# A graph network on one core: the first pass in slots of 60 columns, with larger evictions, two terms for all pieces, and the norm in batches

## The chip, the cores and the metric

One core of one Trainium2 chip runs the whole program. The metric is device time in microseconds of one execution. The engines are TensorE (PE, with its weight loads shown apart as PEld), VectorE (DVE), ScalarE (ACT), GpSimd (POOL) and SyncE (SP, which issues most DMAs). Each runs its own instructions in order and waits for the others by semaphores.

## The reference

A graph has 6250 nodes with 128 features and 206250 directed edges. Cut to what matters:

```python
h = jnp.maximum(_layernorm(x), 0.0)
feat = h * power(clip(deg, 1), -0.5)          # deg: edges that leave a node
x = x + relu(segment_sum(feat[src], dst)) @ W0.T + b0

h = jnp.maximum(_layernorm(x), 0.0)
msg = h[src] @ W_msg.T + b_msg + edge_embed[clip(edge_type, 0, 8)]
x = x + gru_cell(segment_sum(msg, dst), h)    # W_ih, W_hh, b_ih, b_hh
```

So there are two sums over edges. In each, a node's row is the sum of the rows of its sources.

## The kernel before

**Idea.** Nodes are padded to 6272 = 49 blocks of 128. The adjacency matrix (how many edges go from source s to destination d) is built on the chip in bf16, and each sum over edges is a dense product of a table of node rows with it. The first pass builds the matrix, uses it for the first layer and stores it to DRAM (`adj_d`); the second pass reads it back in pieces. If counts at the end show that edges were lost, a general path runs instead; it does not run here.

**Prologue** (0 to about 110 us). Edges are sorted into windows: one window holds two destinations, with up to 64 edges each on one half of the partitions. For every edge the low seven bits of its source (`lo_t`) and its block number (`code_t`) are laid out by window. Degrees and the first norm give the table `tab1`, in seven pieces of 7 blocks (CB = HP = 7). Rows are fp32, and their product with the small integers of the matrix is to be nearly exact, so a row is split into terms. `terms_of` (L737) makes three bf16 terms for piece 0 (`NARROW = 1`, `SPL = 3`) and two fp32r terms for pieces 1 to 6.

**First pass** (L803 to L931). Destinations are taken in chunks (`FRONT`): one of 128 columns and 24 of 256. Its steps:

- `hots` (L343, operations recorded at L336): DVE compares 32 windows (`TW`) with an iota, to `hot_l` (128 x 32 x 128) and `hot_c` (128 x 32 x 50).
- `build` (L812): for each destination PE multiplies the two one-hots on its half of the partitions, 64 rows by 128 by 49 (L823); the result is that destination's column of the matrix, as 128 x 49. Sixteen of them fill a tile `ev` of two PSUM banks, of which there are three buffers. ACT evicts 784 elements per partition at a time to bf16 `adj` (L832).
- `cast` (L893, recorded at L896): pieces 1 to 6 of a finished chunk are cast to fp32r `wide1` (three buffers), on ACT and DVE in turn. Piece 0 is multiplied as bf16 directly.
- `sums` (L780, products at L791): for each block and term one product, 128 x 128 by 256 columns, all 105 into one accumulator `acc`.
- `first_layer` (L837): Relu on ACT (L842), the product with `w0_sb` on PE (L847, in the other half of the accumulator's bank), then on DVE the bias (L851), the residual (L852), the norm's statistics and aggregate (L857, L858), on ACT a square root (L860), on DVE its reciprocal and the shift (L861, L862).

The order on PE, ACT and DVE is written out by hand (`manual_schedule`). While chunk c is built in eight rounds of 32 columns (`RUN`), the products of chunk c - 1 are given out in eight parts: in each round come first the 32 small products, then the evictions, then the casts that `cast_at` names, then a step of the layer, then 13 or 14 long products. At the end of a chunk SP is given the DMA that stores its `adj` (L929); the two `adj` buffers alternate, so chunk c + 2 must wait for that store.

**Second pass** (L937 on). ACT makes the new normalized rows (L954), DVE their terms `tab2` (L955, L956). For 13 blocks of up to 512 destinations (`BACK`) pieces of the matrix are loaded (L1046), cast by ACT (L1050) or DVE (L1057), with row sums for the check (L1030), multiplied (L791), and the GRU's gates (L982, L994) and the rest follow (L987 to L1027).

Of the kernel before, what the change touches and what calls it, by code (L numbers as in the profile page):

```python
# [31 lines left out]
CB = 7  # L32
# [10 lines left out]
TW = 32  # L43
# [8 lines left out]
NARROW = 1  # L52
# [3 lines left out]
def spread(n, k):  # L56

    return [n * (i + 1) // k for i in range(k)]

# [199 lines left out]
def by_matrix(  # L259
# [48 lines left out]
    xs = const.tile([P, NB, H], F32, name="xs")  # L308
    rstd = const.tile([P, NB], F32, name="rstd")
    sh = const.tile([P, NB], F32, name="sh")  # L310
    b0_b = const.tile([P, H], F32, name="b0_b")
# [31 lines left out]
    def hots(w0, place=None):  # L343
        if place is None:
            pool = hot[next(turns) % 2]
            hot_l = pool.tile([P, TW, P], BF16, name="hot_l")
            hot_c = pool.tile([P, TW, CODES], BF16, name="hot_c")
        else:
            hot_l = place[:, : TW * P].rearrange("p (t n) -> p t n", n=P)
            hot_c = place[:, TW * P : TW * (P + CODES)].rearrange("p (t n) -> p t n", n=CODES)  # L350
        one_hot(hot_l, lo_t[:, w0 : w0 + TW, :], iota)
        one_hot(hot_c, code_t[:, w0 : w0 + TW, :], iota_1)
        return hot_l, hot_c
# [13 lines left out]
    with tc.tile_pool(name="pro", bufs=1) as pro, tc.manual_schedule(engines={mybir.EngineType.DVE}):  # L367
# [120 lines left out]
        for k0 in range(0, NT // P + 1, 4):  # L488
# [39 lines left out]

        tab1_p = early.enter_context(tc.tile_pool(name="tab1_p", bufs=1, side="right"))
        tab1 = [  # L530
            tab1_p.tile([P, SPL, CB, H], BF16, name=f"tab1_{q}")
            if q < NARROW
            else tab1_p.tile([P, 2, CB, H], F32R, name=f"tab1_{q}")
# [8 lines left out]
        nc.sync.dma_start(out=b0_b, in_=b0.partition_broadcast(P))  # L542
# [57 lines left out]
        emb_f, bmsg_f, rest = emb_f[:TYPES, :], bmsg_f[:TYPES, :], rest[:TYPES, :]  # L600
        terms = terms[:TYPES, :].bitcast(BF16).rearrange("t (s n) -> t s n", s=SPL)
# [15 lines left out]
        nc.scalar.copy(rest, both_ps[1][:TYPES, : 3 * H])  # L617
# [5 lines left out]
        def fetch(b0_, nb):  # L623
# [14 lines left out]
            inside = wnd.tile([P, 2, GB * ROWS, HALF], BF16, name="inside", bufs=1)  # L638
# [98 lines left out]
        def terms_of(c):  # L737
            f, tab = f_of.pop(c), tab1[c]
            nc.vector.tensor_scalar(tab[:, 0], f, 0.0, None, op0=ALU.max)
            if c < NARROW:  # L740
                nc.vector.scalar_tensor_tensor(f, f, 0.0, tab[:, 0], op0=ALU.max, op1=ALU.subtract)
                nc.vector.tensor_copy(tab[:, 1], f)
                nc.vector.tensor_tensor(tab[:, 2], f, tab[:, 1], ALU.subtract)
            else:
                nc.vector.scalar_tensor_tensor(
                    tab[:, 1], f, 0.0, tab[:, 0].bitcast(F32), op0=ALU.max, op1=ALU.subtract
                )
# [10 lines left out]
        for s in range(SPL):  # L758
# [3 lines left out]
            for g in range(3):  # L762
                at = 32 * g + s * TYPES
                nc.sync.dma_start(out=emb_s[at : at + TYPES, :], in_=terms[:, s, g * H : (g + 1) * H])
# [7 lines left out]
        early_hots.append(hots(TW, first_place[:, NB * P :]))  # L772
# [31 lines left out]
    with tc.tile_pool(name="adj_even", bufs=1, reuse_waits="tile") as adj_even, tc.tile_pool(  # L804
        name="wide1", bufs=3, reuse_waits="tile"
    ) as wide1p, tc.tile_pool(
        name="ev_ps", bufs=3, space=PSUM, reuse_waits="tile"
    ) as evp, tc.manual_schedule(
# [3 lines left out]
        def build(adj, batch, parts):  # L812

            hot_l, hot_c = batch
            made = []
            for part in parts:

                ps = evp.tile([P, 2, 512], F32, name="ev")
                for j in range(8):
                    t = part * 8 + j  # L820
                    for d in range(2):
                        half = slice(d * HALF, (d + 1) * HALF)
                        nc.tensor.matmul(  # L823
                            ps[:, d, j * NB : (j + 1) * NB],
                            hot_l[half, t, :],
                            hot_c[half, t, :NB],
                            start=True,
                            stop=True,
                        )
                made.append((part, ps))  # L830
            for part, ps in made:
                nc.scalar.copy(  # L832
                    adj[:, :, part * 16 : (part + 1) * 16].rearrange("p n (j d) -> p n j d", d=2),
                    ps[:, :, : 8 * NB].rearrange("p d (j n) -> p n j d", n=NB),
                )

        def first_layer(c, acc):  # L837
            d0, nd = FRONT[c]
            nb = nd // P
            blocks = slice(d0 // P, d0 // P + nb)  # L840
# [4 lines left out]
            ps = acc[:, DC : 2 * DC].rearrange("p (b f) -> p b f", f=H)  # L845
            for k in range(nb):
                nc.tensor.matmul(ps[:, k, :], r[:, k * P : (k + 1) * P], w0_sb, start=True, stop=True)  # L847
            yield
            x2 = xs[:, blocks, :]
            y = work.tile([P, DC // P, H], F32, name="y", bufs=1)  # L850
            nc.vector.tensor_tensor(y[:, :nb], ps[:, :nb], b0_b.unsqueeze(1).to_broadcast([P, nb, H]), ALU.add)  # L851
            nc.vector.tensor_add(x2, x2, y[:, :nb])  # L852
            yield
            st = work.tile([P, DC // P, 6], F32, name="st2")
            mv = work.tile([P, DC // P, 2], F32, name="mv2", bufs=3)
            for k in range(nb):
                nc.vector.bn_stats(st[:, k, :], x2[:, k, :])  # L857
                nc.vector.bn_aggr(mv[:, k, :], st[:, k, :])  # L858
            yield
            nc.scalar.activation(rstd[:, blocks], mv[:, :nb, 1], AF.Sqrt, bias=eps)  # L860
            nc.vector.reciprocal(rstd[:, blocks], rstd[:, blocks])  # L861
            nc.vector.scalar_tensor_tensor(  # L862
                sh[:, blocks], mv[:, :nb, 0], -1.0, rstd[:, blocks], op0=ALU.mult, op1=ALU.mult
            )
# [3 lines left out]
        RUN = 32  # L868
        cast_at = {0: (1, 2), 2: (3,), 3: (4,), 4: (5,), 5: (6,)}
        TOTAL = (NARROW * SPL + (NCH - NARROW) * 2) * HP  # L870
        ROUNDS = DC // RUN
        batches = [d // 2 for d in range(0, NP, 2 * TW)]
        ready = early_hots
        made = len(ready)
        adjs = {}
        before, late = None, iter(())
        NC = len(FRONT)
        for c in range(NC + 1):
            d0, nd = FRONT[c] if c < NC else (NP, 0)
            acc, steps = None, iter(())  # L880
            wide = {}
            if c > 0:
                done = adjs.pop(c - 1)
                n = FRONT[c - 1][1]
                acc, steps = sums(
                    n, tab1, lambda q, done=done, wide=wide: wide[q] if q >= NARROW else done[:, q * HP : (q + 1) * HP]
                )
            if c < NC:
                adjs[c] = (adj_even if c % 2 else adj_odd).tile([P, NB, DC], BF16, name="adj") if c > 0 else adj_first
            rounds = nd // RUN if c < NC else ROUNDS  # L890
            ends = spread(TOTAL, rounds)

            def cast(q):  # L893
                wide[q] = wide1p.tile([P, HP, DC], F32R, name="wide1")
# [3 lines left out]
            for r in range(rounds):  # L898
                casts = cast_at.get(r, ()) if c > 0 else ()
                for q in casts:  # L900
                    if r == 0:
                        cast(q)
# [235 lines left out]
```

## Time and profile before

| | us |
|---|---|
| median of 3 runs | 949.86 (947.5 to 950.5) |
| the profiled execution, its own time | 949.22 |
| its span, first to last instruction | 947.1 |
| PE busy | 873.4 (92%) |
| DVE busy | 816.0 (86%) |
| ACT busy | 733.8 (77%) |
| mean granted TensorE clock | 0.965 |

Busy times are unions: instructions of one engine overlap a little, so a duration is longer than the distance from one start to the next. In rows of the timeline a number before the engine is the start and the next the length of a run of equal instructions; brackets give the idle time before it and what ended it. In the table of stretches the columns are the stretch, its length, busy time and count of PE, PEld, DVE, ACT and POOL, then the granted clock, the DMA share and GB/s. A chain row has start, length and what ran.

### The profile page before, as it was taken

The numbers are of one execution on the slowest core, as the hardware profiler recorded it, in microseconds if no ns is written. First come the engines' busy times: TensorE is split into PE (matmuls) and PEld (weight loads), VectorE is DVE, ScalarE is ACT, GpSimd is POOL, SyncE is SP. The second block draws the span as 40 slices with busy tenths as digits, with TensorE's granted clock in tenths as the row PEclk, the third lists the DMA queues.
The fourth block names the chain that finished last, engine by engine and source line by source line (L and its number), as shares of the span: only waits on it lengthen the run. The fifth ranks groups of instructions, "written<-read, shape, count | busy, mean of one in ns | idle before, by whom it ended". The sixth has DMA issues, their size and how long they took to land.

```text
span 947.1 us, 25090 instructions
## 1 busy us (share of the span) xinstructions
PE 873.4 (92%) x11009; PEld 726.6 (77%) x11009; DVE 816.0 (86%) x908; ACT 733.8 (77%) x1397; POOL 40.6 (4%) x78
## 2 busy tenths in 40 slices
PE   3476599999999999999999988999999999999995
PEld 3354399899999989989999987776777777777775
DVE  5879988999999999999999949988988888877754
ACT  3287889999999999999999968766676676666753
POOL 3570000000000000000000000000000000000000
PEclk9579599999999999999999998999999999999998
DMA  9430345576476467557646786777777677666641
GB/s 279 134 118 9 71 134 155 170 205 176 145 205 200 140 186 205 159 162 204 185 138 203 205 288 200 260 252 262 276 242 256 221 272 273 218 239 236 227 117 32
DMA packets 201340, 181.34 MB, mean 191 GB/s; under 512 B 10695, under 2 KB 189627, under 8 KB 201067
## 3 DMA queue, kind: packets, MB, share of 16 engines
q1 hardware_dynamic: 198946, 173.41, 58.8%
q0 software_dynamic: 1664, 4.95, 1.7%
q8 instruction: 88, 1.44, 0.6%
q10 hardware_dynamic: 612, 1.30, 0.4%
q14 instruction: 30, 0.25, 0.1%
HBM read 95.75 MB, written 83.87 MB: 190 GB/s over the span
## 4 chain that ended last, share of the span: by engine, by line
PE 76%; DVE 11%; DMA 6%; ACT 3%; issue 3%; POOL 1%; SPq 0%; DVEq 0%; ACTq 0%
PE acc L791 54%; PE ev L823 10%; DMA piece<-adj_d 3%; DVE wide L1057 3%; PE gate L982 3%; PE gate L994 2%; DVE leave L1030 2%; PE acc L847 2%; DMA adj_d<-adj 1%; DVE fields L648 1%; PE turn L657 1%; ACT wide L1050 1%; DMA dst_i<-in_dst_dram 1%; PE tr L1015 1%; POOL got L627 1%
## 5 line engine op out<-in xcount | busy, mean ns | idle before, releaser
L791 PE MATMUL acc<-wide,tab 128*128 128x256 f32 (+2 forms) x3374 | 591.7, 327 | 4.9 <-DVE tab L956 3.7
L791 PEld LDWEIGHTS acc<-wide,tab 128*128 128x128 f32 x3374 | 492.3, 189 | 62.9 <-issue 10.6
L832 ACT CAST adj<-ev 128x784 bf16<-128x784 f32 x392 | 298.8, 819 | 31.4 <-PE ev L823 28.4
L1050 ACT ACTIVATE wide<-piece 128x512 fp32r<-128x512 bf16 (+1 forms) x336 | 200.8, 601 | 53.4 <-issue 37.6
L336 DVE TENSOR_TENSOR hot_l<-lo_t,iota 128x4096 bf16<-128x4096 bf16 x97 | 221.5, 2283 | 0.5 <-PE ev L823 0.5
L1030 DVE TENSOR_REDUCE leave<-piece 128x7 f32<-128x3584 bf16 (+2 forms) x43 | 154.8, 3601 | 16.4 <-DMA piece<-adj_d 16.3
L896 ACT CAST wide<-adj 128x1792 fp32r<-128x1792 bf16 (+1 forms) x75 | 125.0, 1667 | 3.7 <-PE acc L791 2.9
L823 PE MATMUL ev<-hot_c,hot_l 64*128 64x49 bf16 x6208 | 114.2, 183 | 7.4 <-DVE hot_c L336 4.1
L823 PEld LDWEIGHTS <-hot_l 64*128 64x128 bf16 x6208 | 93.0, 93 | 35.9 <-issue 8.9
L1057 DVE CAST wide<-piece 128x3584 fp32r<-128x3584 bf16 (+2 forms) x43 | 82.5, 1919 | 16.9 <-PE acc L791 16.9
L336 DVE TENSOR_TENSOR hot_c<-code_t,iota 128x1600 bf16<-128x1600 bf16 x97 | 95.4, 983 | 0.0
L896 DVE CAST wide<-adj 128x1792 fp32r<-128x1792 bf16 (+1 forms) x75 | 80.9, 1079 | 9.9 <-ACT adj L832 6.9
L791 PE MATMUL acc<-adj,tab 128*128 128x256 bf16 x525 | 67.2, 277 | 0.0
L1050 ACT ACTIVATION_READ_ACCUMULATOR wide<-piece 128x1 f32 x336 | 63.3, 188 | 0.0
L791 PEld LDWEIGHTS <-tab 128*128 128x128 bf16 x525 | 47.9, 99 | 7.5
L987 ACT COPY sum_sb<-acc 128x512 f32<-128x512 f32 (+2 forms) x13 | 7.3, 562 | 57.0 <-PE acc L791 57.0
L994 PE MATMUL gate<-sum_sb,wsum_sb 128*128 128x512 f32 (+2 forms) x78 | 35.0, 585 | 0.1
L982 PE MATMUL gate<-hT,whh_sb 128*128 128x512 f32 (+2 forms) x78 | 33.8, 569 | 0.0
L657 PE MATMUL turn<-ident_b,fields 128*128 128x128 bf16 x225 | 20.7, 276 | 12.6 <-DVE fields L648 12.6
L657 PEld LDWEIGHTS <-fields 128*128 128x128 bf16 x225 | 19.3, 129 | 14.8 <-DVE fields L648 14.8
L627 POOL DMA_INDIRECT got<-flat,row_i x25 | 26.4, 1055 | 13.3 <-DVE m_dve L682 6.8
L954 ACT ACTIVATE f<-xs,sh,rstd 128x128 f32<-128x128 f32 x49 | 19.5, 481 | 7.0 <-DMA adj_d<-adj 3.4
(163 smaller groups left out, 504.8 us busy)
## 6 DMA issues: line engine op xcount, KB each, us to landing
adj_d<-adj SPq DMA_DIRECT2D x24, 3136.0 KB
piece<-adj_d SPq DMA_DIRECT2D x77, 896.0 KB
piece<-adj_d SPq DMA_DIRECT2D x14, 672.0 KB
piece<-adj_d SPq DMA_DIRECT2D x7, 448.0 KB
out_dram<-res SPq DMA_DIRECT2D x11, 256.0 KB
xs<-in_x_dram SPq DMA_DIRECT2D x6, 448.0 KB
adj_d<-adj SPq DMA_DIRECT2D x1, 1568.0 KB
flat<-turned SPq DMA_DIRECT2D x3, 512.0 KB
```

The lines of the kernel that those rows point to most:

```text
L336: nc.vector.tensor_tensor(to.rearrange("p j (k t) -> p j k t", t=2), twice.unsqueeze(2).to_broadcast([P, n, m // 2, 2]), of[:, :m].rearran ...
L627: nc.gpsimd.indirect_dma_start(out=got[:, b].rearrange("p r f j -> p (r f j)"), out_offset=None, in_=edges_flat, in_offset=bass.IndirectOf ...
L657: nc.tensor.matmul(turns_[i][:, b, :], fields[:, b * ROWS + r, i].rearrange("p d j -> p (d j)"), ident_b, start=(r == 0), stop=(r == ROWS ...
L791: nc.tensor.matmul(acc[:, : 2 * P].rearrange("f (t n) -> f t n", t=2) if twice else acc[:, :nd], tab[:, s, i, :], a[:, i, :P].unsqueeze(1) ...
L823: nc.tensor.matmul(ps[:, d, j * NB : (j + 1) * NB], hot_l[half, t, :], hot_c[half, t, :NB], start=True, stop=True,)
L832: nc.scalar.copy(adj[:, :, part * 16 : (part + 1) * 16].rearrange("p n (j d) -> p n j d", d=2), ps[:, :, : 8 * NB].rearrange("p d (j n) -> ...
L896: make(wide[q][:, :, :n], done[:, q * HP : (q + 1) * HP, :n])
L982: nc.tensor.matmul(ps[:, :nd], whh_sb[:, g * H : (g + 1) * H], hT[:, :nd], start=True, stop=(g == 2))
L994: nc.tensor.matmul(ps[:, :nd], wsum_sb[:, g * H : (g + 1) * H], sum_sb[:, :nd], start=False, stop=True)
L1030: nc.vector.tensor_reduce(leave[:, q * HP : (q + 1) * HP, c], piece, AX.X, ALU.add)
L1050: nc.scalar.activation(pieces[q][:, i, :nd], piece[:, i, :nd], AF.Copy, accum_out=leave[:, q * HP + i, c : c + 1],)
L1057: nc.vector.tensor_copy(pieces[q][:, :, :nd], piece[:, :, :nd])
```

## The change

- **Slots in place of rounds.** Builds are cut by a function `runs()` into evictions of 40 and 20 columns in turn (`EV = (40, 20)`; what is left of a chunk is 16 columns, in the first chunk 8). A slot builds two of them, and nine slots build two chunks of 256 columns: 110 slots in all, with 60 columns, or 56, 36 or 68 where a chunk ends. A chunk's 98 long products are given out over 4.5 slots, from slot 2.5 on, so a slot gets about 22; the last products come in slot 114.
- **Evictions of four and two banks.** A run of 40 goes to a tile of four PSUM banks, a run of 20 to one of two; each has one buffer. The 16 columns use two banks of whichever tile is next.
- **One-hots by slot.** `hots(k)` makes the windows of slot k (30, or fewer where a chunk ends; the second early batch has 34), one slot ahead.
- **Two fp32r terms for all seven pieces.** Piece 0 is now cast too: five of its blocks on DVE and two on ACT; pieces 1, 3, 5 on ACT and 2, 4, 6 on DVE as before. `wide1` has four buffers. A cast stands one slot ahead of its first use.
- **The bias by a product.** `b0` is split into three bf16 terms beside the embedding's (a tenth row of `rest` and `terms`); a product of ones (3 x 128) with them (3 x 256) opens the accumulation to which the products with `w0_sb` add. The addition of `b0_b` and its broadcast DMA go; three small DMAs fetch `b0` and three place its terms.
- **The norm in four batches.** Each chunk only adds the residual and takes statistics into `st2`. After chunks 8, 16, 22 and 24 `norm` makes the factors of all blocks since the last batch.
- The prologue's `inside` moves from a pool of its own into free room of `first_place`.

By the built order, the first 23 of the 49 rows of L954 stand on ACT ahead of the last Relu (4 before), and all loads of the second pass's pieces behind the last store (three of them ahead of it before).

```diff
+EV = (40, 20)
+def runs():
+    made = []
+    for c, (_, n) in enumerate(FRONT):
+        at = 0
+        while at < n:
+            big = len(made) % 2 == 0 or (c == 0 and at == 2 * sum(EV))
+            made.append((c, at, min(EV[0] if big else EV[1], n - at), big))
+            at += made[-1][2]
+    rest = made[5:]
+    return [made[:2], made[2:5]] + [rest[i : i + 2] for i in range(0, len(rest), 2)]
...
-            tab1_p.tile([P, SPL, CB, H], BF16, name=f"tab1_{q}")
-            if q < NARROW
-            else tab1_p.tile([P, 2, CB, H], F32R, name=f"tab1_{q}")
+            tab1_p.tile([P, 2, CB, H], F32R, name=f"tab1_{q}")
...
-            if c < NARROW:
-                nc.vector.scalar_tensor_tensor(f, f, 0.0, tab[:, 0], op0=ALU.max, op1=ALU.subtract)
-                nc.vector.tensor_copy(tab[:, 1], f)
-                nc.vector.tensor_tensor(tab[:, 2], f, tab[:, 1], ALU.subtract)
...
-        name="wide1", bufs=3, reuse_waits="tile"
+        name="wide1", bufs=4, reuse_waits="tile"
-        name="ev_ps", bufs=3, space=PSUM, reuse_waits="tile"
+        name="ev_ps", bufs=1, space=PSUM, reuse_waits="tile"
+    ) as evp, tc.tile_pool(name="ev2_ps", bufs=1, space=PSUM, reuse_waits="tile") as evp2, ...
+        def build(k):
+            hot_l, hot_c = ready.pop(k)
+            t = 0
+            made = []
+            for c, at, n, big in RUNS[k]:
+                ps = (evp if big else evp2).tile([P, 4 if big else 2, 512], F32, name="ev")
+                banks = 4 if n > EV[1] else 2
+                for d in range(n):
+                    half = slice(d % 2 * HALF, (d % 2 + 1) * HALF)
+                    slot = d // banks
+                    nc.tensor.matmul(
+                        ps[:, d % banks, slot * NB : (slot + 1) * NB],
+                        hot_l[half, t + d // 2, :], hot_c[half, t + d // 2, :NB],
+                        start=True, stop=True)
+                t += n // 2
+                made.append((c, at, n, banks, ps))
+            for c, at, n, banks, ps in made:
...
+                nc.scalar.copy(
+                    adjs[c][:, :, at : at + n].rearrange("p n (j d) -> p n j d", d=banks),
+                    ps[:, :banks, : n // banks * NB].rearrange("p d (j n) -> p n j d", n=NB))
...
+            nc.tensor.matmul(
+                ps[:, :nb], ones_s, b0_s.unsqueeze(1).to_broadcast([SPL, nb, H]), start=True, stop=False)
...
-            nc.vector.tensor_tensor(y[:, :nb], ps[:, :nb], b0_b.unsqueeze(1).to_broadcast([P, nb, H]), ALU.add)
-            nc.vector.tensor_add(x2, x2, y[:, :nb])
+            nc.vector.tensor_add(x2, x2, ps[:, :nb])
+            for k in range(nb):
+                nc.vector.bn_stats(st2[:, d0 // P + k, :], x2[:, k, :])
+        def norm(blocks=None):
...
+            nc.vector.tensor_sub(m, part[:, :, 1], part[:, :, 4])
+            nc.vector.tensor_add(v, part[:, :, 2], part[:, :, 5])
+            nc.vector.tensor_mul(m, m, m)
+            nc.vector.scalar_tensor_tensor(v, m, float(H // 4), v, op0=ALU.mult, op1=ALU.add)
+            nc.vector.tensor_add(m, part[:, :, 1], part[:, :, 4])
+            yield
+            nc.scalar.activation(v, v, AF.Sqrt, bias=eps, scale=1.0 / H)
+            yield
+            nc.vector.reciprocal(v, v)
+            nc.vector.scalar_tensor_tensor(m, m, -0.5, v, op0=ALU.mult, op1=ALU.mult)
...
+        EACH = NCH * 2 * HP
+        per = 9 / 4
+        begin = [2.5 + 2 * per * c for c in range(NC + 1)]
...
+                k = int(begin[c] + 2 * per * q / NCH) - 1
+                cast_at.setdefault(k, []).append((c, q))
+        marks = [8, 16, NC - 3, NC - 1]
...
+        def cast(c, q):
+            n = FRONT[c][1]
+            w = wides[c][q] = wide1p.tile([P, HP, DC], F32R, name="wide1")
+            a = adjs[c][:, q * HP : (q + 1) * HP, :n]
+            mine = HP - 2 if q == 0 else HP if q % 2 == 0 else 0
+            if mine:
+                nc.vector.tensor_copy(w[:, :mine, :n], a[:, :mine])
+            if mine < HP:
+                nc.scalar.copy(w[:, mine:, :n], a[:, mine:])
...
+        for k in range(SLOTS):
+            if 1 <= k and k + 1 < len(RUNS):
+                ready[k + 1] = hots(k + 1)
+            if k < len(RUNS):
+                build(k)
+            for c in range(NC):
+                if done_at[c] == k:
+                    store(c)
+            for c, q in cast_at.get(k, ()):
+                cast(c, q)
+            for f in list(under_way):
+                if next(f, "end") == "end":
+                    under_way.remove(f)
+            upto = min(NC * EACH, max(0, round(EACH * (k + 1 - begin[0]) / (2 * per))))
+            run(flow, upto - given)
+            given = upto
```

## The prediction

> **What bounds it now.** I read the table of stretches first, then the timeline of each engine inside the first pass, then the turn from the first pass to the second.
>
> ```profile
> 300.00:400.00 100.00, 100.00 (x1999) 90.91 (x1992) 93.82 (x104) 93.78 (x116) 0.00 (x0) 1.00 0.64 185
> 550.00:600.00 50.00, 42.48 (x254) 38.59 (x254) 38.90 (x47) 33.05 (x80) 0.00 (x0) 0.93 0.79 266
> ```
>
> From 150 to 550 us PE is busy without a gap at a granted clock of 1.00, and DVE and ACT at 94%: three engines near their limits, PE in front. What PE does there:
>
> ```profile
> 302.45 0.58 PE L823 MATMUL ev<-hot_c,hot_l 64*128 64x49 bf16 x32
> 302.96 1.83 PE L791 MATMUL acc<-wide,tab 128*128 128x256 f32 x13
> 304.72 0.58 PE L823 MATMUL ev<-hot_c,hot_l 64*128 64x49 bf16 x32
> ...
> 316.43 1.05 PE L791 MATMUL acc<-adj,tab 128*128 128x256 bf16 x8
> 317.24 0.84 PE L791 MATMUL acc<-wide,tab 128*128 128x256 f32 x5
> 318.01 0.58 PE L823 MATMUL ev<-hot_c,hot_l 64*128 64x49 bf16 x32
> 318.53 0.71 PE L847 MATMUL acc<-w_sb,rl 128*128 128x128 f32 x4
> ```
>
> A round is 32 small products into PSUM (L823), then 13 long ones (L791): 2.265 us, eight to a chunk of 256 columns. The long run without a break further down (554.51) gives 9.72 less a tail of 0.28, over 79: 0.1195 us for an fp32r product. Thirteen of them are 1.55, yet the next small one starts 1.76 after the first. The 32 small ones are 0.40 (0.58 less the 0.18 that one lasts), yet the first long one starts after 0.51. So each round pays 0.21 + 0.11 = 0.31 us (from unrounded starts) for changing kind. A bf16 product is 0.81/8 = 0.102, and L847 adds 0.46. The chunk: 8 x (0.40 + 0.31) + 84 x 0.1195 + 21 x 0.102 + 0.46 = 18.3, and the chain repeats every 18.26.
>
> ```profile
> 301.58 1.70 ACT L896 CAST wide<-adj 128x1792 fp32r<-128x1792 bf16 x1
> 303.17 0.31 ACT L860 ACTIVATE rstd<-mv,eps 128x2 f32<-128x2 f32 x1
> 303.36 1.52 ACT L832 CAST adj<-ev 128x784 bf16<-128x784 f32 x2
> ```
> ```profile
> 299.42 2.28 DVE L336 TENSOR_TENSOR hot_l<-lo_t,iota 128x4096 bf16<-128x4096 bf16 x1
> 301.62 0.98 DVE L336 TENSOR_TENSOR hot_c<-code_t,iota 128x1600 bf16<-128x1600 bf16 x1
> 303.50 0.17 DVE L861 RECIPROCAL rstd<-rstd 128x2 f32<-128x2 f32 x1 [0.90 <-ACT rstd L860]
> 303.79 1.08 DVE L896 CAST wide<-adj 128x1792 fp32r<-128x1792 bf16 x1
> 304.79 0.41 DVE L851 TENSOR_TENSOR y<-acc,b_b 128x256 f32<-128x256 f32 x1
> ```
>
> Instructions on these engines overlap by some 0.1 us, so I count from start to start: one-hots 2.20 + 0.90, DVE cast 1.00, ACT cast 1.59, eviction 0.71. DVE needs 4 x 3.10 + 3 x 1.00 + 0.45 + 0.34 (bias, residual) + 0.83 (statistics) + 0.28 = 17.3 per chunk, and waits 0.9 for ACT's square root: it has nothing to spare either. ACT needs 16 x 0.71 + 3 x 1.59 + 0.28 + 0.20 = 16.6.
>
> The turn, in PE's timeline and in the chain:
>
> ```profile
> 554.51 9.72 PE L791 MATMUL acc<-wide,tab 128*128 128x256 f32 x79
> 566.88 1.23 PE L847 MATMUL acc<-w_sb,rl 128*128 128x128 f32 x4 [2.65 <-ACT rl L842]
> 569.32 0.66 PE L791 MATMUL acc<-wide,tab 128*128 128x384 f32 x1 [1.21 <-DVE tab L955]
> ```
> ```profile
> 550.93 13.88 DMA adj_d<-adj
> 564.92 1.65 ACT f L954 x4
> 597.78 0.02 ACT sum_sb L987
> ```
>
> Products end at 564.2. The new rows (L954) could start only when the last store had landed (564.8); 49 of them take ACT 19 us, DVE makes tables and casts from them, and the first block of the second pass ends at 597.8, 33.6 after the products. From there blocks follow each 29.1 us.
>
> **The change, PE.** A chunk now takes 4.5 slots. Long products: 98 x 0.1195 = 11.7 (was 10.0 + 2.1). Small ones: the same 256, 3.2. Changes of kind: 4.5 x 0.31 = 1.4 (was 2.5). L847's two products 0.46. The bias product is not in the trace: at least 0.10 (a bf16 product of 256 columns), at most 0.31 (as a change of kind); I take 0.12, the near row, as it stands between long products. Sum 16.9. On these rows 1.1 us of the 1.4 come from fewer changes of kind, not from the terms.
>
> **DVE.** 0.521 us per 1000 elements and 0.067 per instruction (from the two one-hot rows): 128 windows x 178 elements, in 9 instructions, 12.5. Casts 3.0, and 0.74 for five of piece 0's seven blocks. One addition 0.45 in place of two, two statistics 0.45; the aggregates and the small factor operations go into four batches (about 0.1 per chunk). Sum 17.1: DVE is now as full as PE, but its wait for the square root falls to four.
>
> **ACT.** 0.837 us per 1000 elements (L896 at 896 and 1792: 0.95 and 1.70). Nine evictions a chunk: 256 x 49 elements 10.5, and 0.054 each, 11.0 (was 11.4). Casts 4.8, two blocks of piece 0 0.5, Relu 0.28: 16.5. That a four-bank read costs as much per element is not in the trace; the bounds are 0.81 (no fixed cost) and 1.04 ns per element (all of 0.819 laid on 784), and I keep 0.84, since the two-bank rows already step across banks.
>
> **The new wait.** The four-bank and the two-bank tile have one buffer each (three before). PE can't refill the 40 columns until ACT has evicted the last 40, and behind that wait on PE stand the slot's 22 long products. A slot is 16.9/4.5 = 3.76. ACT needs 0.87 + 1.69 for the two evictions, and in six of nine slots a cast of 1.59: 4.15. Three such slots follow each other, with a Relu in one: ACT falls 0.39 + 0.67 + 0.39 behind, from a start 0.5 after PE. PE waits once ACT starts more than about 1.3 late (a slot, plus the 0.26 of the small tile, less 2.7). That gives 0.2 to 0.4 in two or three of nine slots, 0.25 to 0.47 per chunk. PE then takes 17.15 to 17.4, DVE alone 17.1. I take 17.35, since neither lets the other run ahead far: 24 chunks x 0.91 = **-21.8**. At best 17.1 (-28); 18.0, if DVE's waits and ACT's add, -6.
>
> **The ends.** The last chunk, without builds, goes from 12.95 to 98 x 0.1195 + 0.6: -0.6. In the prologue two DVE operations on piece 0 (68.07 to 69.8) go, on the chain: -1.7. Piece 0 must now be cast before the first product, and ACT evicts 60 and 68 columns there: +0.7 (0 to 2). The bias rows' DMAs (three and three small ones, for one broadcast) stand on SP behind the last large store of edges or beside it, and land before GpSimd needs them: nothing; exposed, one would cost a landing, 1.9 (the last got<-flat in the chain).
>
> **The turn.** The square-root batches leave ACT's and DVE's queues with three of the seven groups of new rows ahead of the last Relu, and their first wait no longer names the last store. That store leaves with the last eviction, five light slots (15 us) ahead of the end, so it lands about when products end. The pieces of the second pass are issued behind it (three stood ahead of a store before) and land 2 us later each 2.3; DVE wants the first one 5.6 after the products. DVE then has the last residual, its statistics and factors and two copies (4), four tables (1.53 each from start to start), seven casts (1.66 each): about 22, and PE's last group 2.5 and the gates 2: 27 after the products' end, not 33.6. I take **-6** (0, if a landing is late, to -8). After that PE sets 29.1 per block as before.
>
> Sum: -21.8 - 0.6 - 1.7 + 0.7 - 6.0 = -29.4 on the profiled execution's 949.22: 919.8. The median of the runs is 0.6 above it: 920.5, and I say 921.
>
> **Rivals.** *A, the forecast*: 913 to 928, 0.55.
>
> *B, three full engines lock*: each late cast holds PE, PE holds the one-hot buffers, DVE is late in turn, and a chunk takes 17.8 to 18.1. For: 16.9, 17.1 and 16.5 leave no slack. Against: every cast stands a slot ahead of its use, and DVE may run a slot ahead. 24 x 0.3 = 7, with the ends 930 to 943. 0.2.
>
> *C, the changes of kind cost by columns, not by count*: the 0.31 might be waits of the small products. Then only 2.14 - 1.67 - 0.12 per chunk is saved, 17.9: 24 x 0.35 + 7.6 = 16, 934. 0.12. The Trainium skill, "TensorEngine Tiling (Array Packing)", Key Properties, says that a change of tiling mode drains TensorE; by that it goes by count, and the chance of C would be lower still.
>
> *D, slower: the clock.* Half clock for 7 us shows after PE's 2.65 us of idleness at 564 ((1 - 0.93) x 50 / 0.5). If single buffers bring one such stretch into every nine slots, PE loses 3.4 us twelve times: 41, so 962. It decides from idleness somewhere between the 1.42 us that PE sat through before 576.0 at full clock and 2.65; I expect stalls of 0.4. 0.11. The Trainium skill, "TensorE: Matmul & The Clock Gate", in "A second HAM failure mode: psum-queue depth-cycling", tells of a kernel whose small gaps between groups, from cycling through PSUM, made the clock swing. No stretch from 150 to 550 here shows it, with three buffers.
>
> **The numbers.** No change keeps 0.02 (B at its end). The range takes A and B whole and C: from 911 (17.1 per chunk and -8) to 943. Within 0.3%, about what a measurement of this kernel tells from none: 0.02; faster by more 0.87; slower by more 0.11.
>
> **What would show it.** In the new profile: the chain repeats near 34.7 us per two chunks; small products in groups of 56 to 60; PE's waits for evictions some 0.2 to 0.4 each; DVE's wait for the square root gone; some 23 rows of L954's successor ahead of the last Relu; a first block that ends 27 us after the products. Wrong would be: evictions over 1.9 us for 40 columns, a granted clock under 1.00 inside the pass, or PE waiting for one-hots in most slots.

## The result, and the profile after

| | before | after |
|---|---|---|
| median of 16 runs each, taken in turn | 951.17 | 946.77 (945.3 to 949.56) |
| the profiled execution, its own time | 949.22 | 948.31 |
| its span | 947.1 | 946.4 |

The ratio is 0.996 (95% interval 0.9947 to 0.9973): faster by some 4 us, where 29 were forecast, and outside the range of 911 to 943.

The span falls into four stretches, cut at marks that both traces have (us; forecast from the sum, one chunk of the pass counted in the first row):

| stretch | before | after | forecast change | measured |
|---|---|---|---|---|
| start to chunk 1's product with `w0` | 154.2 | 158.5 | -1.9 | +4.3 |
| from there to the end of the last long product | 410.0 | 403.9 | -21.5 | -6.1 |
| from there to the end of the second pass's first block (its copy `sum_sb` starts) | 33.6 | 29.6 | -6 | -4.0 |
| from there to the end | 349.3 | 354.4 | 0 | +5.1 |

The table of stretches of the changed kernel, with the same columns as before, shows the loss at a glance: PE, which had no idle time from 300 to 400, has 6 us of it; the granted clock is 1.00 there, so it is not to blame.

```profile
300.00:400.00 100.00, 93.83 (x1951) 87.92 (x1951) 96.01 (x91) 92.26 (x77) 0.00 (x0) 1.00 0.65 183
550.00:600.00 50.00, 44.07 (x250) 40.13 (x249) 41.12 (x46) 33.97 (x88) 0.00 (x0) 0.90 0.84 276
```

PE's timeline there, and the waits of PE from 120 to 550 us (what waited, for whom: us in total, times, the longest):

```profile
302.70 0.94 PE L843 MATMUL ev<-hot_c,hot_l 64*128 64x49 bf16 x60
304.46 0.26 PE L872 MATMUL acc<-b_s,ones_s 3*128 3x256 bf16 x1 [0.81 <-ACT rl L868]
...
305.12 2.71 PE L811 MATMUL acc<-wide,tab 128*128 128x256 f32 x21
```
```profile
PE acc L872 <- ACT rl L868: 22.2, 22, 1.2
PE ev L843 <- issue: 2.7, 3, 1.9
```

PE stands before the bias product (L872) until ACT's Relu (L868) is done, nearly once per chunk, for about 1 us; of PE's 25 us of idleness in the pass 22.2 are this one wait. Of the wait for ACT's evictions that the prediction priced, nothing is in the list. ACT's timeline in the same slot says why the Relu is late:

```profile
300.72 1.81 ACT L855 CAST adj<-ev 128x1960 bf16<-128x1960 f32 x1
302.40 1.72 ACT L943 CAST wide<-adj 128x1792 fp32r<-128x1792 bf16 x1
303.99 0.42 ACT L868 ACTIVATE rl<-acc 128x256 f32<-128x256 f32 x1
304.27 2.70 ACT L855 CAST adj<-ev 128x980 bf16<-128x980 f32 x2
```

Behind a chunk's last long product ACT's queue holds the next slot's two evictions (2.55 from start to start), a cast (1.59), and only then the Relu (0.28): 4.4 us from the end of that slot's small products. PE reaches the product that needs the Relu one slot later, 3.65 us behind the same point. It mostly waits 0.8 to 1.2, the whole slot behind it waits, and ACT, fed late, waits in turn (L855 for L843: 35.3 us over the span; the same wait, L832 for L823, was 28.4 before). Two chunks take 36.15 us, where the forecast was 34.7 and the kernel before took 36.53.

The turn, with no gap in PE once the second pass has begun:

```profile
554.45 7.96 PE L811 MATMUL acc<-wide,tab 128*128 128x256 f32 x65
...
569.82 17.75 PE L811 MATMUL acc<-wide,tab 128*128 128x384 f32 x84 [4.05 <-DVE sh L900]
```
```profile
592.01 0.48 ACT L1028 COPY sum_sb<-acc 128x384 f32<-128x384 f32 x1 [2.47 <-PE acc L811]
```

Products end at 562.4 and the first block 29.6 later. The last two rows of the table have to be read together: when the first block ended, PE had already started 11 of the second block's products of 512 columns in the kernel before, and 1 in the changed one. Ten of them are 2.3 us (0.227 each), so by PE's work the turn gained 1.7 us and not 4.0, and the second pass lost 2.8 and not 5.1. 23 rows of L995 stand ahead of the last Relu, as forecast; but the first product of the second pass comes only 7.4 us behind the last one of the first, and from 565.5 to 575.8 the granted clock is one half (the 0.90 of the stretch from 550 to 600 is 10 us of it).

### The profile page after: what moved, and what is told of

Same layout as the page of the kernel before. It is cut to its first block, busy times and chain, and to the rows that moved or that the text cites. A ratio compares the mean times of both kernels' runs of the same rounds, so it can differ in the third digit from the quotient of the medians.

```text
span 946.4 us, 24658 instructions
## 1 busy us (share of the span) xinstructions
PE 850.0 (90%) x10859; PEld 716.2 (76%) x10859; DVE 816.0 (86%) x860; ACT 725.8 (77%) x1230; POOL 39.6 (4%) x78
## 4 chain that ended last, share of the span: by engine, by line
PE 66%; ACT 23%; DVE 6%; issue 2%; DMA 2%; POOL 1%; ACTq 0%; SPq 0%; DVEq 0%; POOLq 0%
PE acc L811 47%; ACT adj L855 11%; ACT wide L943 8%; PE ev L843 5%; PE gate L1023 3%; PE gate L1035 3%; PE acc L876 2%; PE turn L681 2%; DVE wide L1098 1%; PE sums L710 1%; DMA dst_i<-in_dst_dram 1%; PE tr L1056 1%; ACT rl L868 1%; PE acc L872 1%; DVE fields L672 1%
## 5 line engine op out<-in xcount | busy, mean ns | idle before, releaser
L811 PE MATMUL acc<-wide,tab 128*128 128x256 f32 (+2 forms) x3724 | 623.8, 323 | 4.1 <-DVE sh L900 4.1
L811 PEld LDWEIGHTS acc<-wide,tab 128*128 128x128 f32 x3724 | 532.2, 190 | 64.4 <-issue 13.4
L855 ACT CAST adj<-ev 128x1960 bf16<-128x1960 f32 (+2 forms) x221 | 282.2, 1339 | 35.3 <-PE ev L843 35.3
L353 DVE TENSOR_TENSOR hot_l<-lo_t,iota 128x3840 bf16<-128x3840 bf16 (+2 forms) x109 | 223.2, 2048 | 0.6 <-PE ev L843 0.6
L943 ACT CAST wide<-adj 128x512 fp32r<-128x512 bf16 (+3 forms) x100 | 140.3, 1417 | 0.4
L941 DVE CAST wide<-adj 128x1280 fp32r<-128x1280 bf16 (+3 forms) x100 | 102.1, 1022 | 27.8 <-ACT adj L855 20.4
L843 PE MATMUL ev<-hot_c,hot_l 64*128 64x49 bf16 x6204 | 102.1, 182 | 6.7 <-DVE hot_c L353 3.6
L843 PEld LDWEIGHTS <-hot_l 64*128 64x128 bf16 x6204 | 88.9, 93 | 20.0 <-DVE hot_c L353 2.6
L353 DVE TENSOR_TENSOR hot_c<-code_t,iota 128x1500 bf16<-128x1500 bf16 (+2 forms) x109 | 97.4, 894 | 0.0
L876 PEld LDWEIGHTS acc<-w_sb,rl 128*128 128x128 f32 x98 | 12.8, 190 | 27.1 <-issue 26.9
L681 PEld LDWEIGHTS <-fields 128*128 128x128 bf16 x225 | 17.8, 121 | 14.0 <-DVE fields L672 9.9
L872 PE MATMUL acc<-b_s,ones_s 3*128 3x256 bf16 (+1 forms) x25 | 6.6, 263 | 22.9 <-ACT rl L868 22.9
L1035 PEld LDWEIGHTS gate<-sum_sb,wsum_sb 128*128 128x128 f32 x78 | 13.7, 189 | 14.1 <-issue 13.0
```

Of the source, the lines that this page charges most:

```text
L353: nc.vector.tensor_tensor(to.rearrange("p j (k t) -> p j k t", t=2), twice.unsqueeze(2).to_broadcast([P, n, m // 2, 2]), of[:, :m].rearran ...
L681: nc.tensor.matmul(turns_[i][:, b, :], fields[:, b * ROWS + r, i].rearrange("p d j -> p (d j)"), ident_b, start=(r == 0), stop=(r == ROWS ...
L811: nc.tensor.matmul(acc[:, : 2 * P].rearrange("f (t n) -> f t n", t=2) if twice else acc[:, :nd], tab[:, s, i, :], a[:, i, :P].unsqueeze(1) ...
L843: nc.tensor.matmul(ps[:, d % banks, slot * NB : (slot + 1) * NB], hot_l[half, t + d // 2, :], hot_c[half, t + d // 2, :NB], start=True, st ...
L855: nc.scalar.copy(adjs[c][:, :, at : at + n].rearrange("p n (j d) -> p n j d", d=banks), ps[:, :banks, : n // banks * NB].rearrange("p d (j ...
L941: nc.vector.tensor_copy(w[:, :mine, :n], a[:, :mine])
```

## The experiments

Theory R: PE waits for the Relu because of its place in ACT's queue. Rival B: three full engines lock through the single PSUM buffers. Later a third question came up, the second pass's 5 us. Ratios are to the kernel before, with 95% intervals; all edits are to the changed kernel unless said.

### The Relu ahead of the casts

```diff
-            for c, q in cast_at.get(k, ()):
-                cast(c, q)
             for f in list(under_way):
                 if next(f, "end") == "end":
                     under_way.remove(f)
+            for c, q in cast_at.get(k, ()):
+                cast(c, q)
```

> The same instructions; in each slot the layer's step (ACT's Relu, DVE's residual and statistics) now stands ahead of the casts instead of behind them. Theory R: in the slot behind a chunk's last long product ACT runs two evictions (2.55), a cast (1.59) and only then the Relu (0.3), 4.4 us from the end of the small products, while PE reaches the product that needs it after one slot, 3.65; so PE waits 0.8 to 1.2 per chunk and ACT, which PE then feeds late, waits in turn. With the Relu at 2.85 this wait goes: two chunks in 34.3 to 34.9 us instead of 36.15, a time of 932 (925 to 936). Rival B, the single PSUM buffers lock three full engines: the wait only moves to the small products, two chunks stay above 35.7, 943 to 950.

Measured: 925.68, ratio 0.9752 (0.9725 to 0.9779). Two undisturbed chunks (no stop of another kind falls into them) take 34.3 to 34.4. PE's and ACT's timeline, and the stretch from 300 to 400:

```profile
310.34 1.08 PE L843 MATMUL ev<-hot_c,hot_l 64*128 64x49 bf16 x60
311.35 0.28 PE L872 MATMUL acc<-b_s,ones_s 3*128 3x256 bf16 x1
```
```profile
310.55 0.41 ACT L868 ACTIVATE rl<-acc 128x256 f32<-128x256 f32 x1
```
```profile
300.00:400.00 100.00, 99.03 (x2089) 93.27 (x2089) 98.59 (x94) 95.98 (x82) 0.00 (x0) 1.00 0.67 189
```

The Relu ends before PE has finished its small products, and L872 follows without a gap. The order of two loops was worth 20 us: the last long product ends at 542.4 instead of 562.4. Both numbers lie in theory R's ranges, at their lower ends.

### The product with the Relu a slot later

```diff
             nc.scalar.activation(r[:, :nd], acc[:, :nd], AF.Relu)
             yield
+            yield
```

> One more slot between the Relu and the products with b0 and w0 (and so one more before the residual); ACT's order is that of the changed kernel, with the Relu behind the cast. Theory R: PE's wait for the Relu goes as well, since PE asks for it 7.3 us behind the small products instead of 3.65: two chunks in 34.3 to 34.9, 932 (925 to 936), with one slot (3.7) more at the very end at most. Rival B: 943 to 950. If the Relu first gains and this one does not, what counts is ACT's order and not PE's wait.

Measured: 942.06, 0.9938 (0.9909 to 0.9967). The wait for the Relu is gone, but undisturbed pairs of chunks take 35.22: PE now waits 9.2 us at the small products for ACT's evictions (18 times, up to 0.6), and some pairs are disturbed on top (37.9, 38.4).

```profile
PE ev L843 <- ACT adj L855: 9.2, 18, 0.6
```

So half of the cost was got back per undisturbed pair, and in the pass as a whole less: the last long product ends at 556.9 instead of 562.4, where the Relu first brought 542.4. Theory R's number failed here. Two more runs were made for that remainder.

### Three tiles of two banks

```diff
-        name="ev_ps", bufs=1, space=PSUM, reuse_waits="tile"
-    ) as evp, tc.tile_pool(name="ev2_ps", bufs=1, ...) as evp2, ...
+        name="ev_ps", bufs=3, space=PSUM, reuse_waits="tile"
+    ) as evp, ...
-                ps = (evp if big else evp2).tile([P, 4 if big else 2, 512], F32, name="ev")
-                banks = 4 if n > EV[1] else 2
+                ps = evp.tile([P, 2, 512], F32, name="ev")
+                banks = 2
```
(each run of 40 columns is cut into two of 20)

> The four-bank and the two-bank tile become three tiles of two banks, used in turn, and each eviction of 40 columns becomes two of 20 (ACT 0.05 more each, 0.2 per chunk); slots, casts and the place of the Relu are unchanged. Rival B: PE may fill the first tile of the next slot while ACT still evicts the last, so the waits between PE and ACT's evictions go and two chunks take 35.0 or less: 930 to 937. Theory R: PE still waits 0.8 for the Relu in every chunk, slightly more as ACT has more to do: two chunks 36 to 36.6, 945 to 952.

Measured: 950.59, 1.001 (0.999 to 1.003). Undisturbed pairs take 36.38 to 36.46, and PE waits 26.2 us for the Relu:

```profile
PE acc L874 <- ACT rl L870: 26.2, 22, 1.4
```

That is theory R's side: the single buffers are not what holds PE. The edit also gives ACT some 0.2 us more to do per chunk, by the expectation's estimate, and nine of PE's waits are 1.42 to 1.44 us here, where the longest of the changed kernel is 1.19. Three of the nine (they end at 171.1, 355.0 and 393.0) were followed by 3.4 us at half clock, which no wait for the Relu in the changed kernel was; those pairs take 38.0.

### Both: the product later, and three tiles

> Both earlier edits at once: the products with b0 and w0 a slot later, and three tiles of two banks. With the products later alone, PE's wait for the Relu was replaced by waits of 0.61 and 0.43 us at the small products for ACT's evictions, twice per two chunks, 35.22 where nothing else disturbed. If those are the price of the single buffers, they go: two chunks 34.4 to 34.9 (ACT has 0.4 more to do), 928 to 935. If ACT is simply late, the wait stays under another name, 35.2 or more and 940 or above.

Measured: 942.74, 0.995 (0.9933 to 0.9967); pairs 35.04 to 35.08, and PE still idles 0.45 and 0.33 at the small products. Against the product later alone the pair is 0.17 shorter, with some 0.4 more of ACT's work in it; the waits for ACT's evictions that are left show that ACT is late there, whatever the buffers.

### The Relu first and the product later

> The Relu ahead of the casts, and the products with b0 and w0 a slot later. With the products later alone, two chunks took 35.2 where nothing else disturbed, and PE waited 0.61 and 0.43 for ACT's evictions. If that comes from taking PE's 0.65 us out of the slot in which ACT is latest (ACT's order up to the next evictions is as long either way), it is the same here: two chunks 35.2, about 940. If the Relu behind the casts is what costs, two chunks take 34.3 to 34.5 as with the Relu first alone, and 925 to 928.

Measured: 938.01, 0.9883 (0.986 to 0.9906); pairs 35.19 to 35.29. Waits of PE from 120 to 520:

```profile
PE ev L843 <- ACT adj L855: 9.7, 18, 0.6
```

The same wait as with the late Relu. A reading that fits these runs: ACT's queue up to the next evictions is as long whether the Relu stands before or behind the cast, so ACT is latest in the slot behind it; with the products in that slot PE has 0.65 us of its own work there, and without them it waits. With the Relu first and the products in place, ACT's lateness is covered by work that PE has anyway.

### The small products in two groups (on top of the Relu first)

```diff
-            for c, at, n, big in RUNS[k]:
+            for i, (c, at, n, big) in enumerate(RUNS[k]):
+                if i == len(RUNS[k]) - 1:
+                    yield
...
-                build(k)
+                for _ in build(k):
+                    run(flow, (upto - given) // 2)
+                    given += (upto - given) // 2
```

> On top of the Relu ahead of the casts: PE's 60 small products of a slot are split, 20, half of the long products, 40, the other half. The same instructions; PE changes kind nine times per chunk instead of four and a half. If a change costs by count, 0.28 to 0.31 us each, PE needs 16.9 + 1.3 = 18.2 per chunk and becomes the bound: two chunks 36.3 to 36.6 instead of 34.4, 949 (944 to 953). If it costs by the number of products, nothing changes: 926 +- 3. PE's waits on its own instructions within the small groups, 4.4 us in all there, should be fewer, as a group is shorter.

Measured: 983.45, 1.0373 (1.0343 to 1.0404); two chunks 39.7. More than forecast, and PE's timeline shows two causes:

```profile
307.51 0.43 PE L845 MATMUL ev<-hot_c,hot_l 64*128 64x49 bf16 x20
307.87 1.56 PE L811 MATMUL acc<-wide,tab 128*128 128x256 f32 x11
309.36 0.68 PE L845 MATMUL ev<-hot_c,hot_l 64*128 64x49 bf16 x40
309.97 1.58 PE L811 MATMUL acc<-wide,tab 128*128 128x256 f32 x11
311.48 0.43 PE L845 MATMUL ev<-hot_c,hot_l 64*128 64x49 bf16 x20
...
313.51 1.20 PE L811 MATMUL acc<-wide,tab 128*128 128x256 f32 x8 [1.06 <-ACT wide L945]
```

A slot without waits takes 311.48 - 307.51 = 3.97 instead of 3.65: one more change each way costs 0.32, so the price goes by count, as the main term of the sum had it (0.31). By the Trainium skill, "TensorEngine Tiling (Array Packing)", Key Properties, a change of tiling mode drains TensorE; a cost per change, here 0.32, fits that. The rest, 2.6 us per pair, is waits for ACT's casts (0.83, 1.06 and 0.64 in the order of the pair): half of a slot's long products now come half a slot earlier and ask for them sooner. As expected, PE's waits on "issue" within the small groups are gone.

### Dummy products at the turn (on top of the Relu first)

```diff
+        idle = evp.tile([P, 4, 512], F32, name="ev")
+        for i in range(36):
+            nc.tensor.matmul(idle[:, 0, :DC], tab1[NCH - 1][:, 0, 0, :],
+                             wides[NC - 1][NCH - 1][:, 0, :], start=True, stop=True)
```

> On top of the Relu ahead of the casts: behind the last product with w0, 36 products of 256 columns into a free tile that nothing reads (4.3 us) keep PE busy until the second pass's first product, so that it idles under 1 us there. If idleness closes the clock, the stretch of half clock at the turn (547.7 to 554.5) goes and the first block ends 2.5 us earlier: 923 against 925.7 (921 to 926). If the clock falls for another reason, or the first block waits for DVE and not for PE, nothing changes, within 1 us.

Measured: 932.06, 0.9838 (0.981 to 0.9866), 6 slower than without (8 by the two ratios). It tells nothing of the clock: the order of the second pass's first operations, which is not written out by hand, came out differently with these products in, with tables and copies ahead of DVE's first cast. The first product came at 554.1 instead of 549.2, and the idle time and the half clock (6.8 us) only moved. Inconclusive.

### One batch of the norm instead of four (on top of the Relu first)

```diff
-        marks = [8, 16, NC - 3, NC - 1]
+        marks = [NC - 1]
```

> The Relu ahead of the casts, and the norm's factors in one batch behind the last chunk instead of four. What the batches were to bring at the turn goes: none of the new rows can stand ahead of the last Relu, all 49 (0.385 each from start to start) come behind it, so that ACT's rows and no longer DVE set the first block: it ends 33 us behind the last long product instead of 28.9, as in the kernel before (33.6). In the pass DVE loses some 24 short operations of 0.1 to 0.2 us in front of other work, 1 to 3 us in all if DVE sets it. Sum: 927 (925 to 930). If the turn is set elsewhere, 923 to 925.

Measured: 934.05, 0.9842 (0.9811 to 0.9872). The first block ends 37.0 us behind the products (29.1 with four batches), with half clock for 13.7 us there (6.8). The batches' place is worth 8 us at the turn, more than the 4 I expected, so the time lies above the range given (925 to 930); the pass, with 34.41 per pair on average in both, gains nothing from fewer short operations.

### The second pass's 5 us, and place in memory

A product of 512 columns starts 0.227 us behind the one before it in the kernel before and 0.232 in the changed one (medians, 620 to 890 us). In the view by line and form the mean length shows it, here before, after, and with the Relu first and the shift for the second pass alone (the last diff below):

```profile
L791 PE MATMUL acc<-wide,tab 128*128 128x512 f32 x670 | 164.1, 401 | 0.0
```
```profile
L811 PE MATMUL acc<-wide,tab 128*128 128x512 f32 x657 | 164.3, 405 | 0.0
```
```profile
L811 PE MATMUL acc<-wide,tab 128*128 128x512 f32 x648 | 158.7, 400 | 0.0
```

> The kernel before, unchanged, for a second profile. In the profiles so far a product of 512 columns in the second pass starts 0.227 us behind the one before it in the kernel before, and 0.232 in the changed kernel and its variants. If that comes from the changed program, 0.227 stands here again; if it comes from chip or hour, 0.232, and the second pass takes the same time in both kernels. The first small product of the first pass, at 98.7 before and at 99.9, 96.8, 96.5 and 96.3 in the four others, shows how far the prologue differs between executions: I expect it between 96 and 100.

Measured: 948.4 in one run, 0.227 again: it is the program. The first small product came at 99.2. In the twelve experiments on the changed kernel it came at 96.2 to 100.2, and at 104.4 in the kernel before with the shift below.

The shift by 96 bytes, on top of the Relu first:

```diff
-    st2 = const.tile([P, NB, 6], F32, name="st2")
+    st2 = const.tile([P, NB * 6 + 24], F32, name="st2")[:, : NB * 6].rearrange("p (b s) -> p b s", s=6)
```

> On top of the Relu ahead of the casts: 24 unused floats per partition behind st2, so that all that lies behind it in SBUF moves by 96 bytes. The instructions and their order are the same. In the kernel before, the second pass's table (the stationary operand) starts at byte 49632, its cast piece (the moving one) at 186336: both 96 above a multiple of 128. The changed kernel's new tiles moved the table to 50816, 0 above one. Theory P (place in memory): the product of 512 columns goes back from 0.232 to 0.227 us, 13 blocks of 98 give 6 us, and the time is 919.5 (917 to 922) against 925.7. If the place is without effect, 0.232 stays and 925.7 +- 1.5.

Measured: 926.86, 0.9735 (0.9701 to 0.9769). The product fell to 0.227 and the second pass (first product to end) from 376.4 to 372.1; but the first pass's product of 256 columns rose from 0.1177 to 0.1197 (mean from start to start), 34.43 per undisturbed pair, and the time stayed.

The opposite, in the kernel before (`rstd` 8 floats longer):

> The kernel before with 8 unused floats per partition behind rstd, nothing else: its second pass's table moves from byte 49632 to 49664, which is a multiple of 128. Theory P: a product of 512 columns takes 0.232 instead of 0.227 and the kernel loses 5 to 6 us (ratio 1.006). Without such an effect the ratio is 1.000.

Measured: 953.35, 1.0022 (1.0000 to 1.0044), 0.2325 for the product. Less than half of the expected loss of 5 to 6 us. The first pass gained 1.4 from the same shift (36.41 per two chunks instead of 36.53), and behind the second block's first product PE idled 3.4 us in all instead of 6.6 (5.7 in the second profile of the kernel before), so that not all of the longer products shows in the time.

One block of piece 0 more on ACT, with the shift:

> The shifted kernel, and one of piece 0's seven blocks more cast by ACT (three) and one less by DVE (four). DVE, busy 98.6% in the stretch from 300 to 400 us with the Relu first, has 0.13 less per chunk, ACT, 96%, 0.21 more. If DVE sets the pass now, two chunks take 0.2 less and the time falls by 2 to 3 us; if ACT's lateness sets it, the waits of the small products for ACT's evictions grow and it rises by 2 to 5.

Measured: 927.07, 0.9742 (0.9708 to 0.9777): no difference in the time. In the profiles the pass got longer, 34.57 to 34.59 per undisturbed pair instead of 34.43, and 1.9 us from chunk 1 to the last long product. DVE is busy 96.3% from 300 to 400 instead of 97.5%, but waits more for ACT (5.9 us instead of 2.7 from 250 to 500). Neither sign came: the pair got no shorter, and PE's waits for ACT's evictions did not grow (0.4 us from 250 to 500, 0.6 without the edit). What sets the pass there stays open.

The shift for the second pass alone, first with the Relu first, then in the changed kernel itself:

```diff
+        tab2a.tile([P, 24], F32, name="shift")
         whh_sb = gru_a.tile([P, 3 * H], F32, name="whh_sb", bufs=1)
```

> The Relu ahead of the casts, and the shift of 96 bytes only from the second pass's pools on (24 unused floats ahead of its tables); the first pass's tiles stay where the changed kernel has them. With the shift for all, the second pass's product fell from 0.232 to 0.227 us and that pass from 376.4 to 372.1 us (first product to end), but in the first pass the product of 256 columns rose from 0.1177 to 0.1197, and the time stayed. If both readings are effects of place, this kernel has the better of each: two chunks as with the Relu first (34.4), the second pass in 372, ratio to the kernel before 0.971 against 0.975, 921 (919 to 923).

Measured: 922.74, 0.971 (0.9681 to 0.9738), the fastest kernel here, 25.4 us below the 948.18 of the kernel before in the same runs. Both readings held: 0.227, and 34.3 for an undisturbed pair.

> The changed kernel with 24 unused floats per partition ahead of the second pass's tables, nothing else. If the place is worth what it was with the Relu first (ratio 0.971 against 0.975, second pass 4 us shorter), the product of 512 columns takes 0.227 and the ratio to the kernel before falls from 0.996 to 0.9915 (0.989 to 0.994). Without effect it stays at 0.996.

Measured: 942.01, 0.993 (0.9906 to 0.9955), 0.227. The interval overlaps that without the shift a little; the product's length does not. The stretch from the first block to the end falls from 354.4 to 351.4, so the place is worth 3.0 of the table's 5.1; the 2.1 that are left are about the second block's work that the kernel before had done ahead of the mark (2.3).

## Why the prediction was wrong

**The step that failed** is "the new wait", with 17.35 us per chunk and -21.8 as its result. The step asked who waits behind a late ACT, found the next slot's evictions, and priced 0.25 to 0.47 per chunk. It computed that ACT needs 4.15 for two evictions and a cast against a slot of 3.76, and counted the Relu as work of ACT's, but did not ask who waits for it behind that cast: PE's next layer product. The two numbers were in hand: 0.87 + 1.69 + 1.59 + 0.28 = 4.4 against 3.76 gives 0.7 per chunk. In the kernel before the Relu stood two rounds, 4.5 us, ahead of its product in the program. It ended 1.7 us before the product started:

```profile
316.48 0.40 ACT L842 ACTIVATE rl<-acc 128x256 f32<-128x256 f32 x1
```

(the product is the prediction's row at 318.53). Inside the pass PE never waited for it, so no row showed a wait; the order of ACT's queue in the diff pointed at it. Measured: 18.08 per chunk. With the Relu moved, 17.2, and the end of the first pass comes 21.8 us earlier than before; the forecast's terms up to that point (-21.8 - 0.6 - 1.7 + 0.7) give -23.4.

**Confirmed** by the changed kernel and that run: PE's 16.9 per chunk (36.15 less 2.1 of idleness, halved: 17.0), the evictions at 0.87 and 1.69, the one-hots, and that the three engines could all be kept near full. Changes of kind by count: confirmed with 0.32 by the two groups; rival C falls.

**Rival B** named 17.8 to 18.1 per chunk and so came nearest in size, up to 943 in time, but its mechanism is not it: three buffers gained nothing, and with the Relu first the same single buffers go with 34.3 per pair.

**Rival D**, the clock, did not come in the changed kernel. Waits of 0.8 to 1.2 in nearly every chunk left the granted clock at 1.00. It was not far off: with three tiles, three of nine waits of 1.42 to 1.44 were followed by half clock, which cost about 1.5 us each. By the Trainium skill, "TensorE: Matmul & The Clock Gate", "A second HAM failure mode: psum-queue depth-cycling", small gaps between groups made the clock swing in another kernel; the changed kernel's waits of up to 1.2 do not show it.

**The ends.** The prologue was right within what executions differ by. What the table books as +4.3 at the start is 1.2 of that, and in chunk 1 a stop of 1.89 us inside a group of small products with 3.4 us at half clock behind it, which no term foresaw:

```profile
158.17 0.18 PE L843 MATMUL ev<-hot_c,hot_l 64*128 64x49 bf16 x1 [1.89 <-issue]
...
158.96 4.25 PE L811 MATMUL acc<-wide,tab 128*128 128x256 f32 x21
```

**The turn** had its mechanism right (one batch costs 8 us more) and its size too large: 29.6 behind the products, not 27, and by PE's work a gain of 1.7 where 6 were forecast. The step took DVE's 22 us as the bound; PE's 84 products without a gap, from 7.4 us on, set it, six of their microseconds at half clock.

**"After that PE sets 29.1 per block as before"** failed by the place of the tables, which the change's new small tiles moved: late in the pass a block takes 29.2 before, 29.6 in the changed kernel and 29.2 in it with the shift. No row of the profile of before had a price for that.

Of the 28.7 us between forecast and profile, the Relu's place explains 20.0, and the turn and the second pass together 7.1 (by the table 2.0 and 5.1, by PE's work 4.3 and 2.8). The 1.6 that are left are the end of the products with the Relu first, 542.4 instead of 540.8: chunk 1's product with `w0` comes 3.3 later there than forecast (155.6, not 152.3), behind the same kind of stop (1.86 us), and the pass from there on is 1.7 shorter than forecast.

## What to carry to other kernels

When an order written by hand is cut into coarser slots, lay out for each engine's result both times from the same event: when the producing engine gets to it behind everything that its slot puts ahead, and when the consumer asks; a short operation that another engine waits for goes ahead of long ones that have a slot to spare. A wait taken away at the consumer can come back at the next thing that the same late engine owes, so move the producer first. And a change that adds a few small tiles moves all that lies behind them: compare the length of untouched instructions in both profiles before a difference is booked to the edit.

## What the runs showed of the hardware

- An fp32r product of 512 columns takes 0.227 or 0.232 us, and one of 256 columns 0.1177 or 0.1197, by where its tiles lie in SBUF. A shift of 32 or 96 bytes turned it each time. With the second pass's table 96 bytes above a multiple of 128 it was 0.227, with the table on a multiple 0.232 (the addresses are those of the expectations); the shift of 96 bytes that shortened the second pass's products lengthened the first pass's, so no rule follows, and which of the tiles counts stays open.
- With groups of 60 small products PE stops now and then in or behind such a group for 0.2 to 2.2 us, released by nothing that the profile shows ("issue"); a stop of 1.4 to 2.0 stands between 152 and 159 us in all of these kernels. The kernel before, with groups of 32, has none, and with groups of 20 and 40 there were none. In the changed kernel PE stops at 156.28, and a 16 KB transfer of the instruction queue (q8) runs from 155.7 to 156.6. The other stops fit: in the twelve kernels with groups of 60 there are 81 of 0.15 us or more between 120 and 535 us, and each ends 2.20 to 2.69 us after the start of such a transfer, whatever its own length, where in the changed kernel transfers start 3.3 to 10.6 us apart. So PE seems to wait for its instructions there; no run changed their loading, so this is read from the times alone.
- The stop of 1.89 us in the changed kernel was followed by 3.4 us at half clock; its waits of up to 1.19 in nearly every chunk were not. The length of the idle time does not decide it alone: in the run with three tiles three of nine waits of 1.42 to 1.44 were followed by half clock, and in the run with three tiles and the product later a stop of 1.00 was (at 280.7) and one of 2.17 was not (at 334.8). The Trainium skill, "TensorE: Matmul & The Clock Gate", "Why this matters for your kernels", advises against gaps over some 3 us; here 1.0 to 1.9 was enough at times.
